# An LSTM on one core: weights in 512 KB transfers, x and h0 behind them, another order of the set-up

## The chip, the cores and the metric

The kernel runs on one core of a Trainium2 chip. The metric is device time in microseconds (us) of one execution. The engines that matter are TensorE (PE in the profile; its weight loads are PEld), VectorE (DVE), ScalarE (ACT), GpSimd (POOL) and SyncE (SP). ACT, SP and POOL also issue DMA transfers, each into a queue of its own[...]. SBUF is the core's working memory, PSUM the memory that TensorE adds its products into, HBM the memory that holds inputs and outputs.

## The reference

An LSTM with 512 hidden values runs over 512 time steps for 16 sequences. Its output is added to its input.

```python
xW = jnp.einsum('ntd,dg->ntg', x, Wx) + b          # x: (16, 512, 512), Wx: (512, 2048)

def step(carry, xw_t):
    prev_h, prev_c = carry
    a = xw_t + prev_h @ Wh                          # Wh: (512, 2048)
    i = sigmoid(a[:, :H]); f = sigmoid(a[:, H:2*H])
    o = sigmoid(a[:, 2*H:3*H]); g = tanh(a[:, 3*H:])
    next_c = f * prev_c + i * g
    next_h = o * tanh(next_c)
    return (next_h, next_c), next_h

_, hs = scan(step, (h0, 0), swapaxes(xW, 0, 1))     # h0: cond_1024, (16, 512)
out = x + swapaxes(hs, 0, 1)
```

All data are float32.

## The kernel before

**Layout.** The 2048 gate columns are cut into four blocks of 32 partitions each (index `j`), and the 512 inputs of a product into four chunks of 128 (index `c`). A chunk of `Wx` or `Wh` is a tile slice of 128 partitions x 2048 columns of float32, 1 MB. `Wx` is used as it is. `Wh` is cut into three float16 parts, `wq[0]`, `wq[1]`, `wq[2]`, whose scaled sum is close to the float32 value, so that the recurrent products run in float16.

**Set-up (lines 333 to 466).** The weights are loaded by `load_w` (line 124): four transfers of 256 KB for a chunk of Wh, issued in turn by SP and ACT, and eight of 128 KB for a chunk of Wx, by SP and POOL. POOL's queue has, ahead of its share of Wx, the first tile of x (`load_xs(0, nc.gpsimd)`, eight transfers of 32 KB), h0 (four) and the bias broadcast over partitions (eight). A semaphore is reused after eight transfers of a kind of queue, and the ninth is issued only when the first has landed.

`bound(c)` finds, for each partition, a bound of the absolute values of chunk `c` of Wh, on DVE for chunks 0 to 2 (line 381) and on ACT for chunk 3 (line 379, an absolute value with a running sum). `scales(h)` makes the scale factors of chunks 2h and 2h + 1 in small DVE operations. `split(n, k)` works on half chunk `n` (0 to 7), in five operations: k = 0, ACT makes the first part (line 414); k = 1, DVE its remainder `r1` (line 417); k = 2, ACT the second part (line 421); k = 3, DVE the remainder `r2` (line 424); k = 4, ACT the third part (line 426). The scheduler is manual: each engine executes its instructions in the order in which the program writes them, and waits where a semaphore says so.

`turn_x(q)` transposes the x of two time steps (a pair, `q`) on DVE. `put_bias(q)` copies the bias into a PSUM bank `xb` on ACT (line 154). `project(q, c)` adds the product with chunk `c` of Wx there on TensorE (line 163). `seed(t, h)` scales the projected values of step `t` from `xb` into the PSUM bank of its gates, on ACT (line 173). `zeros` (line 368) is a product of zeros: 8 of them clear the PSUM banks at the start, and 16 stand as fillers after the first projections.

**Order around the change.** On DVE the transposes of x pairs 0 and 1 and of h0 stand first, then `bound(0)`, `bound(1)`, `scales(0)` and the splits; `bound(2)` is at n = 1, `bound(3)` and `scales(1)` at n = 2. In each pass of the loop over `n`, `split(n, 4)` is the last operation. The two bias copies are at n = 3 and 4, the projections of pairs 0 and 1 at n = 4 in PE's order, the seeds of step 0 at n = 6.

**Steps (lines 468 to 503).** Step 0 uses float32 products with Wh (`first_products`, line 199), each later one the float16 parts (`products`, line 186), with the order of work written out in `STEP_PE` and `STEP`. Each step also projects half of a pair that is needed two to four steps later.

Of the kernel before, what the change touches and what calls it, by code (L numbers as in the profile page):

```python
# [7 lines left out]
FP = mybir.dt.float32  # L8
# [6 lines left out]
P = 128  # L15
Q = 32
# [15 lines left out]
def lstm_residual(ctx: ExitStack, tc: tile.TileContext, x, h0, wx, wh, b, out):  # L32
# [26 lines left out]
    nc = tc.nc  # L59
    N, T, D = x.shape  # L60
    H = h0.shape[1]
    NJ = H // P
    NK = D // P
    G = 4
    U = P // 2
    GU = G * U
# [8 lines left out]
    const = ctx.enter_context(tc.tile_pool(name="const", bufs=1))  # L75
# [38 lines left out]
    parts = [  # L114
        [const.tile([P, 2, 5 * N], HP, tag=f"parts{h}{i}", name=f"parts{h}{i}") for i in range(2)]
        for h in range(2)
    ]
    gates = [
        [psum.tile([P, G * P], FP, tag=f"g{h}{i}", name=f"gates{h}{i}") for i in range(2)]
        for h in range(2)  # L120
    ]
    xb = [psum.tile([P, G * P], FP, tag=f"xb{i}", name=f"xb{i}") for i in range(NXB)]

    def load_w(dst, w, c, dmas, parts=1):


        n = G * H // parts
        for j in range(NJ):
            r0 = j * P + c * Q
            for e in range(parts):  # L130
                a = parts - 1 - e
                dmas[j % 2].dma_start(  # L132
                    out=dst[j * Q : (j + 1) * Q, c, a * n : (a + 1) * n],
                    in_=w[r0 : r0 + Q, e * n : (e + 1) * n],
                )

    xs = {}

    def load_xs(s, dma=nc.sync):

        xs[s] = xsp.tile([P, XP, P], FP, tag="xs", name=f"xs_{s}")
        for j in range(NJ):
            for r in range(S2):
                p0 = j * Q + r * N
                dma.dma_start(
                    out=xs[s][p0 : p0 + N],
                    in_=x[:, s * XB + r : (s + 1) * XB : S2, j * P : (j + 1) * P],
                )
# [4 lines left out]
    def put_bias(q):  # L153
        nc.scalar.copy(xb[q % NXB], bias)  # L154

    def turn_x(q):
        s, i = divmod(q, XP)
        xT[q] = xtp.tile([P, NK, Q], FP, tag="xT", name=f"xT_{q}")
        nc.vector.transpose(xT[q].rearrange("p c m -> p (c m)"), xs[s][:, i])

    def project(q, c):
        for j in range(NJ):
            nc.tensor.matmul(  # L163
                xb[q % NXB][j * Q : (j + 1) * Q],
                lhsT=xT[q][:, c],
                rhs=wx_j[:, c, j],
                start=False,
                stop=(c == NK - 1),
                skip_group_check=True,
            )  # L170

    def seed(t, h):
        nc.scalar.mul(  # L173
            gates[h][t % 2][:, :GU].rearrange("p (g u) -> p g u", g=G),
            xb[t // 2 % NXB].rearrange("p (g h u) -> p h g u", g=G, h=2)[:, h],
            mask[:, t % 2 : t % 2 + 1],
        )
# [155 lines left out]
    h_in = work.tile([P, P], FP, tag="h_in", name="h_in", bufs=1)  # L333
    hT0 = work.tile([P, NK, Q], FP, tag="hT0", name="hT0", bufs=1)
    warm = const.tile([1, 1], FP, tag="warm", name="warm")
    for c in range(NK):
        load_w(wh_sb, wh, c, (nc.sync, nc.scalar))
    load_xs(0, nc.gpsimd)
    nc.vector.memset(zero, 0.0)
    nc.vector.memset(h_in, 0.0)  # L340
    for j in range(NJ):
        nc.gpsimd.dma_start(out=h_in[j * Q : j * Q + N], in_=h0[:, j * P : (j + 1) * P])
    b_j = b.rearrange("(o e g j w) -> j e o g w", o=1, e=2, g=2, j=NJ)
    for j in range(NJ):
        for e in range(2):
            nc.gpsimd.dma_start(
                out=bias[j * Q : (j + 1) * Q, (1 - e) * GU : (2 - e) * GU].rearrange(
                    "p (g w) -> p g w", g=2
                ),
                in_=b_j[j, e].broadcast_to([Q, 2, P]),  # L350
            )
    for c in range(NK):
        load_w(wx_sb, wx, c, (nc.sync, nc.gpsimd), 2)
    load_xs(1)

# [11 lines left out]
    def zeros(bank, start):  # L367
        nc.tensor.matmul(  # L368
            bank, lhsT=zero[:, :P], rhs=zero, start=start, stop=start, skip_group_check=True
        )  # L370


    for bank in xb + gates[0] + gates[1]:
        zeros(bank, True)

    def bound(c):
        if c == NK - 1:
            junk = tmp.tile([P, G * H], HP, tag="junk", name="junk", bufs=1)
            nc.scalar.activation(junk, wh_sb[:, c], AF.Abs, accum_out=amax[:, c : c + 1])  # L379
        else:  # L380
            nc.vector.tensor_reduce(
                amax[:, c : c + 1],
                wh_sb[:, c],
                mybir.AxisListType.X,
                ALU.max,
                apply_absolute_value=True,
            )

    def scales(h):


        nc.vector.tensor_tensor(
            top[:, h : h + 1], amax[:, 2 * h : 2 * h + 1], amax[:, 2 * h + 1 : 2 * h + 2], ALU.max
        )
        t = top[:, h : h + 1].bitcast(I32)
        e, inv = bits[:, h, 0:1], bits[:, h, 1:2]
        nc.vector.tensor_scalar(
            inv.bitcast(I32), t, EXP, EXP, ALU.bitwise_and, ALU.bitwise_xor
        )
        nc.vector.tensor_scalar(e.bitcast(I32), t, EXP, None, ALU.bitwise_and)  # L400
        nc.vector.tensor_scalar(RS2[h], inv, 2.0**12, 0.5, ALU.mult, ALU.min)
        nc.vector.tensor_scalar(RS[h], inv, 2.0**13, 1.0, ALU.mult, ALU.min)
        nc.vector.tensor_scalar(S[h], e, 2.0**-14, 1.0, ALU.mult, ALU.max)
        nc.vector.tensor_scalar(RSL[h], RS[h], 1.0 / LO, None, ALU.mult)
# [3 lines left out]
    def split(n, k):  # L408

        c, e = divmod(n, 2)  # L410
        w = wh_sb[:, c, e * GH : (e + 1) * GH]
        f = [q[:, c, (1 - e) * GH : (2 - e) * GH] for q in wq]
        if k == 0:
            nc.scalar.mul(f[0], w, RS2[c // 2])
        elif k == 1:
            r1[n] = tmp.tile([P, GH], FP, tag="r1", name=f"r1_{n}")
            nc.vector.scalar_tensor_tensor(  # L417
                r1[n], w, RS[c // 2], f[0], ALU.mult, ALU.subtract
            )
        elif k == 2:  # L420
            nc.scalar.copy(f[1], r1[n])  # L421
        elif k == 3:
            r2[n] = tmp.tile([P, GH], FP, tag="r2", name=f"r2_{n}")
            nc.vector.tensor_tensor(r2[n], r1[n], f[1], ALU.subtract)  # L424
        else:
            nc.scalar.mul(f[2], r2[n], LO)  # L426

    NH = 2 * NK
    for q in range(2):
        turn_x(q)  # L430
    nc.vector.transpose(hT0.rearrange("p c m -> p (c m)"), h_in)
    bound(0)
    bound(1)
    scales(0)
    split(0, 0)
    split(1, 0)
    split(0, 1)
    for n in range(NH):
        if n == 1:
            bound(2)  # L440
        if n == 2:
            bound(3)
            scales(1)
        if n + 1 < NH:
            split(n + 1, 1)
        split(n, 2)
        split(n, 3)
        if n + 2 < NH:
            split(n + 2, 0)
        split(n, 4)  # L450
        if n in (3, 4):
            put_bias(n - 3)
        if n == 4:
            for c in range(NK):
                for q in range(2):
                    project(q, c)

            for _ in range(16):
                zeros(xb[3], False)
        if n == 6:  # L460
            for h in range(2):
                seed(0, h)
    for h in range(2):
        seed(1, h)
    put_bias(2)
    turn_x(2)

    for t in range(T):
        s, ti = divmod(t, XB)
        q, half = divmod(t + 4, 2)  # L470
# [12 lines left out]
        for op in STEP.split():  # L483
            name, h = op.split("_")
# [47 lines left out]
```

## Time and profile before

| | us |
|---|---|
| median of 3 runs (lowest, highest) | 2313.13 (2312.34, 2313.43) |
| profiled execution: its own time | 2313.33 |
| profiled execution: span | 2311.4 |
| busy in the span: PE, DVE, ACT, POOL | 2249.4, 1952.7, 1840.0, 136.1 |
| first projection that PE does not interrupt again | starts at 55.60 |
| last of Wh, first tile of x, last of Wx landed | 24.9, 22.6, 45.9 |
| one time step later on (matmuls of line 186 and 163) | 4.36 |

Times are from the start of the span, which is the first instruction of the program. The profile's page is a summary of one execution: busy time of each engine, the span in 40 slices with the busy share in tenths, the DMA queues (q1 is SP's, q10 is ACT's, q0 is POOL's), the chain of work that ended last, and the costliest groups of instructions. The trace behind it can be asked for a stretch: the chain in order of time, the timeline of instructions, or the DMA traffic by queue. In a timeline the value in brackets is how long the engine was idle before the instruction, and what ended it. "Record" is one matmul as the trace has it; a float32 product of `project` leaves two.

### The profile page before, as it was taken

The page shows a single profiled execution, that of the slowest core. Times are in us where ns is not written, and L with a number is a line of the kernel's source. Part 1 is how long each engine was busy: PE and PEld are TensorE (multiplying, and loading weights), DVE is VectorE, ACT ScalarE, POOL GpSimd, SP SyncE. Part 2 cuts the span into 40 slices and gives each one's busy share as a digit, 9 for nine tenths or more (in the row PEclk, how much of TensorE's full clock was granted, in tenths as well). Part 3 has the DMA queues.
Part 4 walks back from the last instruction along what each step waited for, and adds up shares of the span by engine and source line. Part 5 has one row for each costly group of instructions (what it writes and reads, how often), then busy time and mean ns, then how long its engine had stood idle before and what let it go on. Part 6 is the DMA issues. An engine that isn't in the chain of part 4 may idle for free.

```text
span 2311.4 us, 137693 instructions
## 1 busy us (share of the span) xinstructions
PE 2249.4 (97%) x57400; PEld 1572.5 (68%) x57400; DVE 1952.7 (84%) x11812; ACT 1840.0 (80%) x7962; POOL 136.1 (6%) x300
## 2 busy tenths in 40 slices
PE   1999999999999999999999999999999999999997
PEld 0677667766776677667776776677767776777675
DVE  4688888888888888888888888888888888888887
ACT  4788888888888888888888888888888888888887
POOL 3000000000000000000000000000000000000000
PEclk9999999999999999999999999999999999999999
DMA  7000000000000000000000000000000000000000
GB/s 164 4 21 22 14 21 22 13 22 22 13 22 22 13 22 19 16 22 20 15 22 19 16 22 17 18 22 17 18 22 15 20 22 14 21 22 13 22 17 12
DMA packets 84974, 51.10 MB, mean 22 GB/s; under 512 B 17473, under 2 KB 82561, under 8 KB 83841
## 3 DMA queue, kind: packets, MB, share of 16 engines
q1 hardware_dynamic: 82432, 37.52, 7.1%
q8 instruction: 452, 7.41, 1.4%
q0 software_dynamic: 1408, 2.66, 0.6%
q10 hardware_dynamic: 512, 2.13, 0.4%
q14 instruction: 170, 1.38, 0.2%
HBM read 25.46 MB, written 16.78 MB: 18 GB/s over the span
## 4 chain that ended last, share of the span: by engine, by line
PE 97%; DMA 2%; DVE 0%; ACT 0%; issue 0%; ACTq 0%; POOLq 0%; POOL 0%; SPq 0%
PE gates L186 58%; PE xb L163 38%; DMA wh_sb<-in_L_cond_Wh_dram 1%; DMA wx_sb<-in_L_cond_Wx_dram 1%; DMA xs<-in_x_dram 0%; PE gates L199 0%; PE xb L368 0%; DVE r L424 0%; ACT wq L426 0%; ACT junk L379 0%; ACT wq L421 0%; DVE r L417 0%; DVE gt L222 0%; ACT xb L154 0%; ACTq L132 0%
## 5 line engine op out<-in xcount | busy, mean ns | idle before, releaser
L186 PEld LDWEIGHTS <-parts 128*32 128x32 f16 x49056 | 1307.0, 96 | 368.7 <-DVE parts L282 297.9
L186 PE MATMUL gates<-wq,parts 128*32 128x256 f16 x49056 | 1449.0, 273 | 4.2 <-DVE parts L282 4.1
L163 PE MATMUL xb<-wx_sb,xT 128*32 128x512 f32 x8192 | 978.0, 594 | 48.9 <-ACT xb L154 48.9
L222 DVE STREAM_TRANSPOSE gt<-gates 128x192 f32<-128x192 f32 x1024 | 391.8, 383 | 233.0 <-PE gates L186 170.3
L163 PEld LDWEIGHTS xb<-wx_sb,xT 128*32 128x32 f32 x8192 | 264.1, 110 | 355.4 <-issue 303.8
L256 ACT ACTIVATE gc<-pre 128x32 f32<-128x32 f32 x1022 | 234.4, 229 | 274.3 <-DVE pre L229 261.1
L173 ACT ACTIVATE gates<-xb,mask 128x256 f32<-128x256 f32 x1024 | 450.3, 440 | 1.1 <-PE xb L163 1.1
L264 ACT ACTIVATE os<-so,sc 128x32 f32<-128x32 f32 x1024 | 328.9, 321 | 16.7
L286 ACT COPY parts<-parts 128x32 f16<-128x32 f16 x1022 | 214.3, 210 | 131.9 <-DVE parts L282 131.9
L229 DVE SCALAR_TENSOR_TENSOR pre<-gt 128x96 f32<-128x96 f32 x1024 | 253.7, 248 | 0.0
L258 ACT ACTIVATE sif<-pre 128x64 f32<-128x64 f32 x1024 | 245.6, 240 | 0.0
L324 POOL TENSOR_TENSOR ob<-hb,xs 128x128 f32<-128x128 f32 x256 | 116.8, 456 | 2149.6 <-DVE hb L323 1909.6
L222 DVE STREAM_TRANSPOSE gto<-gates 128x64 f32<-128x64 f32 x1024 | 229.6, 224 | 0.0
L274 ACT ACTIVATE tch<-gc 128x32 f32<-128x32 f32 x1024 | 226.6, 221 | 0.2
L262 ACT ACTIVATE so<-preo 128x32 f32<-128x32 f32 x1024 | 226.4, 221 | 0.0
L296 DVE SCALAR_TENSOR_TENSOR parts<-rem,parts 128x32 f16<-128x32 f32 x1022 | 196.2, 192 | 35.5
L229 DVE SCALAR_TENSOR_TENSOR preo<-gto 128x32 f32<-128x32 f32 x1024 | 192.2, 188 | 17.6
L288 DVE SCALAR_TENSOR_TENSOR parts<-parts,hist 128x32 f16<-128x32 f16 x1022 | 191.9, 188 | 17.7
L266 DVE TENSOR_TENSOR pr<-sif,gc 128x64 f32<-128x64 f32 x1022 | 204.7, 200 | 0.0
L282 DVE TENSOR_TENSOR parts<-os,tch 128x32 f16<-128x32 f32 x1022 | 196.4, 192 | 0.0
L272 DVE TENSOR_TENSOR gc<-pr 128x32 f32<-128x32 f32 x1024 | 192.2, 188 | 0.0
L276 DVE SCALAR_TENSOR_TENSOR hist<-os,tch 128x32 f32<-128x32 f32 x1024 | 188.8, 184 | 0.3 <-ACT tch L274 0.3
(45 smaller groups left out, 741.2 us busy)
## 6 DMA issues: line engine op xcount, KB each, us to landing
xs<-in_x_dram SPq DMA_DIRECT2D x504, 32.0 KB, 2.2
out_dram<-ob SPq DMA_DIRECT2D x504, 32.0 KB, 1.9
wh_sb<-in_L_cond_Wh_dram ACTq DMA_DIRECT2D x8, 256.0 KB, 10.6
wh_sb<-in_L_cond_Wh_dram SPq DMA_DIRECT2D x8, 256.0 KB, 10.6
wx_sb<-in_L_cond_Wx_dram SPq DMA_DIRECT2D x16, 128.0 KB, 5.9
wx_sb<-in_L_cond_Wx_dram POOLq DMA_DIRECT2D x16, 128.0 KB, 6.8
xs<-in_x_dram POOLq DMA_DIRECT2D x8, 32.0 KB, 13.2
bias<-in_L_cond_b_dram POOLq DMA_DIRECT2D x8, 32.0 KB, 5.5
```

The costliest lines, as they stand in the source:

```text
L163: nc.tensor.matmul(xb[q % NXB][j * Q : (j + 1) * Q], lhsT=xT[q][:, c], rhs=wx_j[:, c, j], start=False, stop=(c == NK - 1), skip_group_chec ...
L173: nc.scalar.mul(gates[h][t % 2][:, :GU].rearrange("p (g u) -> p g u", g=G), xb[t // 2 % NXB].rearrange("p (g h u) -> p h g u", g=G, h=2)[: ...
L186: nc.tensor.matmul(g[j * Q : (j + 1) * Q, :GU], lhsT=a[:, cc, k * N : (k + 2) * N], rhs=wq_j[i - 1][:, 2 * kh + cc, h, j], start=False, st ...
L222: nc.vector.transpose(gt.rearrange("p b m -> p (b m)"), gates[h][t % 2][:, b0 * Q : b1 * Q])
L229: nc.vector.scalar_tensor_tensor(pre.rearrange("p g (c n) -> p (g c) n", c=2), gt[:, :, (1 - t % 2) * N : (2 - t % 2) * N], 1.0 / LO, gt[: ...
L256: nc.scalar.activation(gc[h][:, 0], v["pre", h][:, 0], AF.Tanh)
L258: nc.scalar.activation(new("sif", t, h, [P, 2, 2 * N]), v["pre", h][:, 1:3], AF.Sigmoid)
L262: nc.scalar.activation(new("so", t, h, [P, 2 * N]), v["preo", h][:, 0], AF.Sigmoid)
L264: nc.scalar.mul(new("os", t, h, [P, 2 * N]), v["so", h], S[h])
L266: nc.vector.tensor_tensor(new("pr", t, h, [P, 2, 2 * N]), v["sif", h], gc[h], ALU.mult)
L274: nc.scalar.activation(new("tch", t, h, [P, 2 * N]), gc[h][:, 1], AF.Tanh)
L286: nc.scalar.copy(slots(t, h, 2), slots(t, h, 0))
```

## The change

`load_w` now loads two chunks with one call: for Wh eight transfers of 512 KB in all (a transfer holds a block of 32 partitions with two rows each), for Wx sixteen of 256 KB. Blocks j = 0, 1 go through the first queue given, j = 2, 3 through the second. x's first tile and h0 move from POOL's queue to SP's, behind Wh and ahead of SP's Wx. POOL loads a row of the bias first, and then the bias tile and its Wx.

The banks `xb[0]` to `xb[2]` get their bias by 24 products of a row of ones with the bias row, instead of a product of zeros and, later, a copy on ACT. From pair 3 on `put_bias` is used as before.

`bound(1)` moves to ACT (it has the running sum there), `bound(3)` to DVE. `bound(2)` moves ahead by one pass. `split(n, 4)` is issued one pass later, after `split(n + 1, 3)`. The transposes of x (pairs 0 to 2) and of h0 move from the front of DVE's order to the end of pass n = 3. The steps' code is unchanged.

```diff
-    def load_w(dst, w, c, dmas, parts=1):
+    def load_w(dst, w, c0, dmas, parts=1):
         n = G * H // parts
-        for j in range(NJ):
-            r0 = j * P + c * Q
-            for e in range(parts):
-                a = parts - 1 - e
-                dmas[j % 2].dma_start(
-                    out=dst[j * Q : (j + 1) * Q, c, a * n : (a + 1) * n],
-                    in_=w[r0 : r0 + Q, e * n : (e + 1) * n],
-                )
+        for j in range(2):
+            for q, dma in enumerate(dmas):
+                r = w[(2 * q + j) * P + c0 * Q :][: 2 * Q].rearrange("(c u) f -> u c f", u=Q)
+                p = slice((2 * q + j) * Q, (2 * q + j + 1) * Q)
+                for e in range(parts):
+                    a = parts - 1 - e
+                    dma.dma_start(
+                        out=dst[p, c0 : c0 + 2, a * n : (a + 1) * n],
+                        in_=r[:, :, e * n : (e + 1) * n],
+                    )
...
-    for c in range(NK):
+    brow = const.tile([1, G * H], FP, tag="brow", name="brow")
+    ones = const.tile([1, Q], FP, tag="ones", name="ones")
+    for c in (0, 2):
         load_w(wh_sb, wh, c, (nc.sync, nc.scalar))
-    load_xs(0, nc.gpsimd)
+    load_xs(0)
     nc.vector.memset(zero, 0.0)
     nc.vector.memset(h_in, 0.0)
+    nc.vector.memset(ones, 1.0)
     for j in range(NJ):
-        nc.gpsimd.dma_start(out=h_in[j * Q : j * Q + N], in_=h0[:, j * P : (j + 1) * P])
+        nc.sync.dma_start(out=h_in[j * Q : j * Q + N], in_=h0[:, j * P : (j + 1) * P])
+    nc.gpsimd.dma_start(out=brow, in_=b.rearrange("(o f) -> o f", o=1))
...
-    for c in range(NK):
+    for c in (0, 2):
         load_w(wx_sb, wx, c, (nc.sync, nc.gpsimd), 2)
...
-    for bank in xb + gates[0] + gates[1]:
+    for bank in gates[0] + gates[1] + xb[3:]:
         zeros(bank, True)
+    for bank in xb[:3]:
+        for e in range(2):
+            for j in range(NJ):
+                nc.tensor.matmul(
+                    bank[j * Q : (j + 1) * Q, (1 - e) * GU : (2 - e) * GU],
+                    lhsT=ones,
+                    rhs=brow.rearrange("p (e g j w) -> p e j g w", e=2, g=2, j=NJ)[:, e, j],
+                    start=(e == 0),
+                    stop=False,
+                    skip_group_check=True,
+                )
...
-        if c == NK - 1:
+        if c == 1:
             junk = tmp.tile([P, G * H], HP, tag="junk", name="junk", bufs=1)
...
-    for q in range(2):
-        turn_x(q)
-    nc.vector.transpose(hT0.rearrange("p c m -> p (c m)"), h_in)
     bound(0)
     bound(1)
     scales(0)
     split(0, 0)
+    split(0, 1)
     split(1, 0)
-    split(0, 1)
     for n in range(NH):
-        if n == 1:
+        if n == 0:
             bound(2)
         if n == 2:
             bound(3)
             scales(1)
         if n + 1 < NH:
             split(n + 1, 1)
         split(n, 2)
         split(n, 3)
+        if n:
+            split(n - 1, 4)
         if n + 2 < NH:
             split(n + 2, 0)
-        split(n, 4)
-        if n in (3, 4):
-            put_bias(n - 3)
+        if n == 3:
+            for q in range(3):
+                turn_x(q)
+            nc.vector.transpose(hT0.rearrange("p c m -> p (c m)"), h_in)
...
+    split(NH - 1, 4)
     for h in range(2):
         seed(1, h)
-    put_bias(2)
-    turn_x(2)
```

## The prediction

> **What bounds the kernel now.** The page's first two parts say that TensorE is full from about slice 2 on, at full clock; the recurrence is its own bound.
>
> ```profile
> PE 2249.4 (97%) x57400; PEld 1572.5 (68%) x57400; DVE 1952.7 (84%) x11812; ACT 1840.0 (80%) x7962; POOL 136.1 (6%) x300
> PE   1999999999999999999999999999999999999997
> ```
>
> None of the 511 later time steps is edited, so only the set-up ahead of them can move. The chain of waits in order of time (start us, us, what) shows where it ends:
>
> ```profile
> 54.01 1.06 ACT wq L426
> 55.06 0.49 ACT xb L154
> 55.60 8.32 PE xb L163 x56
> 63.92 4.18 PE xb L368 x16
> 68.10 6.29 PE gates L199 x128
> 74.39 1.72 PE xb L163 x16
> ```
>
> From 55.60 on PE hardly rests again. What stood last before it is ACT's bias copy, queued behind the Wh splits. So the end moves by as much as the end of `first_products` (74.39) moves, and I compute that one time. The timeline (start, us, engine, line, [idle before <- releaser]) says why the splits were late:
>
> ```profile
> 22.68 0.50 DVE L159 STREAM_TRANSPOSE xT<-xs 128x128 f32<-128x128 f32 x2 [20.65 <-DMA xs<-in_x_dram]
> 26.15 0.31 DVE L431 STREAM_TRANSPOSE hT<-h_in 128x128 f32<-128x128 f32 x1 [2.97 <-DMA h_in<-in_cond_dram]
> 26.39 4.45 DVE L381 TENSOR_REDUCE amax<-wh_sb 128x1 f32<-128x2048 f32 x2
> 50.20 1.06 ACT L426 ACTIVATE wq<-r 128x1024 f16<-128x1024 f32 x1 [0.24 <-DVE r L424]
> 54.01 1.06 ACT L426 ACTIVATE wq<-r 128x1024 f16<-128x1024 f32 x1 [0.24 <-DVE r L424]
> ```
>
> DVE sat until 26.1 for x and h0, although the trace's landings have Wh's chunks 0 and 1 at 14.4 and all of Wh at 24.9. After that each half chunk took 3.8 us (50.20 to 54.01), as ACT waits on DVE for `split(n, 4)`. Behind these stands the transfer of Wx, hidden today: its last piece lands at 45.9.
>
> [...] In 36 to 44 us POOL's Wx (two 4 KB pieces per engine and transfer) ran against SP's x (four of 512 B):
>
> ```profile
> q0 software_dynamic: 467, 1.29, 82.4%
> q1 hardware_dynamic: 786, 0.32, 26.7%
> ```
>
> 1.29 against 0.32 MB is 4 to 1, the ratio of whole transfers per engine and not of pieces (8 to 1). [...] here the sum stays at 201 to 251 GB/s in the stretches 2 to 24, 24 to 30, 30 to 36 and 36 to 44 us, whoever issues. [...] projection records are 0.214 us apart from 55.60 to 59.9 and 0.107 us after; in `first_products` 0.053 us until 73.5 and 0.027 after.
>
> **The change, part by part.**
>
> *Wh's arrival.* 4.19 MB now goes as eight transfers of 512 KB, all issued at once. Before, 4.64 MB moved in 2 to 24 us (211 GB/s). POOL's queue again holds small transfers meanwhile (8 KB of bias row and 8 of 32 KB, where it had 8 x transfers of 32 KB), so I put chunks 0 and 1 at 13.5 and chunks 2 and 3 at 24.0 (23 to 25).
>
> *Bounds and splits.* DVE no longer waits for x and h0. The reduction of chunk 0 (2.2) runs beside ACT's of chunk 1 (1.89 + 0.19), and `scales(0)` and the first split operations are done by about 20. Then `bound(2)` stands in DVE's order ahead of `split(1, 1)`, and waits for the second half of Wh: all of DVE is queued behind it, and ACT's `split(1, 2)` with it. From 24.0 DVE runs, in its new order: two reductions at 2.2, `scales(1)` at 0.7, four r1 at 1.19 (line 417), four r2 at 1.14 (line 424), 14.4 in all. The first `turn_x` ends at 24.0 + 14.4 + 0.3 = 38.7. ACT keeps up: `split(n - 1, 4)` now uses an r2 made one half earlier, and three ACT operations at about 1.0 make 3.0 us per half where it was 3.8. ACT reaches `seed(0, ...)` at about 46.5. Its last splits stand behind the seeds and end near 52; step 1's products want them after 59, so they cost nothing. Were that cover gone, they would cost up to 3 us.
>
> *Bias by products.* Two copies of 0.49 leave the path, a third was off it. The 24 small matmuls need only a row of the bias, and run in PE's idle time (some 20 us before 38); unhidden they would be 48 records at 0.05 to 0.11 (the 0.053 of 128 columns at half clock, up to doubled for 256), 2.4 to 5.3 us. The row is POOL's first transfer; the first of x there landed at 9.9 today. I take nothing. The `ones` memset is a row of 32 values among idle DVE time.
>
> *x, h0 and Wx.* x[4..7] wait for landings of Wh's second half, h0[0..3] for x[0..3], SP's first four Wx pieces for x[4..7], the last four for h0. So SP's Wx stands behind 0.26 MB of x and 0.03 MB of h0 in short pieces. Against POOL's Wx, x took 8 us for 0.32 MB above[...]. I put the start of SP's Wx at 31 to 36. POOL's half flows from about 25 with the rest of the bandwidth. What is left after 24 us is 4.19 + 0.29 = 4.5 MB; at 251 to 201 GB/s it ends between 42 and 46.4, so 45. The half that projection's chunks 0 and 1 need from SP (1.05 MB) lands at 39.5 (start 31, shared at 125) to 41.3 (start 36, alone at 200): I take 40.3.
>
> *PE.* It starts at the later of 38.7 and 40.3: 40.3. Projection of pairs 0 and 1 is 8 + 56 = 64 records. [...] 24 x 0.214 + 40 x 0.107 = 9.4, ending at 49.7 (8.6 to 10.3 with the ends). Chunks 2 and 3 are wanted at 45.4 or later, so their landing at 45 is just hidden; each us beyond 46 costs a us. Seeds need the projection of pair 0 only and end under the 16 filler products, as before. Fillers and `first_products` took 4.18 + 6.29 = 10.5, nearly all of the second at half clock; fully warm they would take 16 x 0.217 + 128 x 0.027 = 6.9. [...] I take 9.4. `first_products` ends at 59.1.
>
> *Sum.* 74.4 - 59.1 = 15.3 us. The profiled execution took 2313.33 (span 2311.4 and 1.9 around it), near the median of 2313.13. 2313.3 - 15.3 = 2298.0.
>
> **Rivals.**
>
> *The forecast* (0.67): end of `first_products` at 59.1, own range from start 39.5, 8.6 and 8.0 (56.1) to start 41.5, 10.3 and 10.5 (62.3): 2295.0 to 2301.2.
>
> *Wx becomes the bound* (0.15): POOL's half runs first, SP's then goes alone through one queue from 38 at 150 GB/s, and lands at 52. Then the last 32 records (3.4 warm, 6.9 if the clock fell) and 9.4 follow: 65 to 68, so 2304 to 2307; smaller delays make 2301 to 2304. For it: x and h0 stand ahead of SP's Wx. Against: one queue with POOL's bias beside it moved 184 GB/s (page of 24 to 30 us: 1.11 MB in 6 us).
>
> *More is won* (0.10): PE starts by 39[...], and `first_products` runs warm: 39 + 8.6 + 6.9 = 54.5, a gain of 19.9, 2293.4; about 2291 to 2295.
>
> *Nothing measurable* (0.05): the gain is eaten where Wx's last piece lands at 57 (57 + 3.4 + 9.4 = 69.8, under 4.6 us won). That is 4.5 MB at 136 GB/s, below every stretch of the trace before 44 us.
>
> *Slower* (0.03): SP's chain of waits serialises. If x, h0 and Wx, 20 transfers, went one after the other at the 2.2 us from issue to landing that the page has for x, the last would land at 24 + 44 = 68, and `first_products` would end at 68 + 3.4 + 9.4 = 80.8: 2319.7. It decides from a last landing of 66 on. Against: eight semaphores go round, so up to eight are in flight, as today.
>
> **How the numbers follow.** 0.2% (4.6 us) is about what this measurement can tell from no change. The forecast, the larger gain and the late Wx are all faster by more: 0.92; same 0.05; slower 0.03. The range of 2293.0 to 2304.5 holds the forecast's 0.67, about 0.07 of the larger gain and 0.08 of the late Wx.
>
> **What would show it.** Right: the first reduction starts at 13 to 15, the reduction of chunk 2 at 23 to 25, xT at 38 to 40; PE's first projection at 39.5 to 41.5 without a wait on ACT; ACT's line 444 waits no longer for DVE by 0.24; `first_products` ends at 56 to 62, and the steps after it take 4.36 us each as now. Wrong: a PE wait on Wx between projection records, Wh's second half after 27 (POOL's Wx cutting in), SP idle between its Wx pieces, or a change in the later steps, which I hold at nothing because neither their instructions nor their order are touched.

## The result and the profile after

The changed kernel takes 2297.58 us (median of 6 runs, 2294.09 to 2298.14), the kernel before 2313.06 beside it: a ratio of 0.9931, 95% interval 0.9918 to 0.9944, or 15.5 us won. The forecast was 2298.0.

The execution that was profiled is the fastest of the six: 2294.09, span 2291.7. Its granted clock is 0.999 over the span, and 0.998 in the five others; that difference becomes the main theme of the first experiments. The first two parts of its page:

```profile
PE 2249.4 (98%) x57445; PEld 1572.7 (69%) x57445; DVE 1952.7 (85%) x11813; ACT 1838.1 (80%) x7959; POOL 127.2 (6%) x281
PE   4999999999999999999999999999999999999997
```

PE is busy for the same 2249.4 us as before, in a span that is 19.7 us shorter. So what went is, on balance, idle time, in the first slice (4 tenths busy instead of 1). The chain of waits in order of time:

```profile
22.44 9.42 DMA xs<-in_x_dram
31.86 0.02 issue
31.88 6.03 DMA wx_sb<-in_L_cond_Wx_dram
37.91 0.14 issue
38.05 9.27 PE xb L165 x64
47.31 3.56 PE xb L374 x16
50.87 3.63 PE gates L201 x128
54.50 1.72 PE xb L165 x16
```

What stands last before PE's unbroken run is now a transfer of Wx at 37.9, no longer ACT's bias copy at 55.1. `first_products` (L201) ends at 54.5 instead of 74.4. From the first `products` of step 2 to the end of the span it is 2231.1 us (2291.7 - 60.55), against 2230.9 before (2311.4 - 80.45): the steps did not change.

DVE's timeline shows where the time came from:

```profile
12.77 2.29 DVE L399 TENSOR_REDUCE amax<-wh_sb 128x1 f32<-128x2048 f32 x1 [10.69 <-DMA wh_sb<-in_L_cond_Wh_dram]
22.26 2.29 DVE L399 TENSOR_REDUCE amax<-wh_sb 128x1 f32<-128x2048 f32 x1 [4.07 <-DMA wh_sb<-in_L_cond_Wh_dram]
...
36.79 0.69 DVE L161 STREAM_TRANSPOSE xT<-xs 128x128 f32<-128x128 f32 x3
```

The first reduction starts at 12.8 instead of 26.4, with the landing of Wh's first half. DVE then waits once more, for Wh's second half, and works without a break to the transposes of x at 36.8. Between 24 and 32 us the DMA view has POOL's Wx against SP's x and h0:

```profile
q0 software_dynamic: 439, 1.41, 86.5%
q1 hardware_dynamic: 531, 0.28, 20.4%
```

POOL's queue took five times the bytes of SP's. Its last piece of Wx landed at 33.2, all of x at 31.9 and h0 at 33.5, and only then came SP's share of Wx, one 256 KB piece every 1.28 us to the last at 43.2.

### The profile page after: what moved, and what is told of

It reads as the page before. It is cut to its first block, busy times and chain, and to the rows that moved or that the text cites. A ratio compares the mean times of both kernels' runs of the same rounds, so it can differ in the third digit from the quotient of the medians.

```text
span 2291.7 us, 137735 instructions
## 1 busy us (share of the span) xinstructions
PE 2249.4 (98%) x57445; PEld 1572.7 (69%) x57445; DVE 1952.7 (85%) x11813; ACT 1838.1 (80%) x7959; POOL 127.2 (6%) x281
## 4 chain that ended last, share of the span: by engine, by line
PE 98%; DMA 2%; DVE 0%; issue 0%; ACTq 0%; POOLq 0%; POOL 0%; SPq 0%
PE gates L188 59%; PE xb L165 38%; DMA wh_sb<-in_L_cond_Wh_dram 1%; DMA xs<-in_x_dram 0%; DMA wx_sb<-in_L_cond_Wx_dram 0%; PE gates L201 0%; PE xb L374 0%; ACTq L134 0%; DVE gt L224 0%; DVE preo L231 0%; DVE pre L231 0%; DVE parts L284 0%; DVE gto L224 0%; POOLq L544 0%; POOL ob L326 0%
## 5 line engine op out<-in xcount | busy, mean ns | idle before, releaser
L188 PEld LDWEIGHTS <-parts 128*32 128x32 f16 x49056 | 1307.1, 96 | 368.8 <-DVE parts L284 298.8
L188 PE MATMUL gates<-wq,parts 128*32 128x256 f16 x49056 | 1449.2, 273 | 4.2 <-DVE parts L284 4.2
L258 ACT ACTIVATE gc<-pre 128x32 f32<-128x32 f32 x1022 | 234.7, 230 | 274.7 <-DVE pre L231 261.9
```

Source lines behind the costliest of these rows:

```text
L188: nc.tensor.matmul(g[j * Q : (j + 1) * Q, :GU], lhsT=a[:, cc, k * N : (k + 2) * N], rhs=wq_j[i - 1][:, 2 * kh + cc, h, j], start=False, st ...
L258: nc.scalar.activation(gc[h][:, 0], v["pre", h][:, 0], AF.Tanh)
```

## The experiments

There are twelve experiments. e1 to e4, e5 to e8 and e9 to e12 were each measured beside runs of the kernel before, whose medians were 2312.9, 2315.41 and 2315.06; so kernels of different groups are compared by their ratio to it. They are told here by the question that they answer.

### The clock: fillers and the first step's products

**e1, the changed kernel again**, without an edit.

> The changed kernel again, unedited, to see whether its profiled execution (2294.09, below its median of 2297.58) differs from the others in the clock. Clock theory: most executions fall back to half clock while the 16 filler products run, so that first_products takes about 6.3 us instead of 3.6; median 2297.6, and a profile of such an execution has first_products at 5 to 6.3 us and its end near 58, all else as in the first profile. Start theory: the spread comes from the start of the projections (38 in the first profile, 41 in others), with first_products at 3.6 in each.

Median 2296.81 (2295.65 to 2298.84), ratio 0.9931 (0.9918 to 0.9943). The profile is now of the slowest execution, 2298.84. Its chain:

```profile
37.63 9.77 PE xb L165 x64
47.40 4.42 PE xb L374 x16
51.82 6.05 PE gates L201 x128
57.87 1.72 PE xb L165 x16
```

The projections start 0.4 earlier than in the first profile and end at 47.4, as there. The same 16 fillers then took 4.42 instead of 3.56, and the same 128 records of `first_products` 6.05 instead of 3.63. In the kernel before these two rows are 4.18 and 6.29, and its granted clock is 0.50 from 66.7 to 73.5, over the last fillers and most of `first_products`; in the first profile it is 1.00 from 47.3 to 54.5. Of the 3.9 us between the two spans 3.3 are in these two rows (10.47 against 7.19). In the kernel before, the records of `first_products` were 0.053 us apart at half clock and 0.027 after it; with that factor of two I estimate, from the 3.3 us, about 6.6 us of half clock in e1. The clock theory holds, the start theory falls.

**e2, no fillers.**

```diff
-            for _ in range(16):
-                zeros(xb[3], False)
```

> The changed kernel without the 16 filler products of zeros, which only pass time. In the first profile the seeds of step 0 end at 47.3, with the projections, so nothing has to be waited for. Clock theory: 3.6 us of fillers go, and first_products always runs at full clock, which most executions lack: end near 51, median 2290.5 (7 below 2297.6). Start theory: only the 3.6 us go: 2294.0. Rival on the fillers: they cover a wait for the seeds, the time stays within 1 us of 2297.6.

Median 2291.07 (2290.63 to 2291.28), ratio 0.9905 (0.9892 to 0.9919): 5.7 below e1, nearer to the clock theory's 7 than to the 3.6 of the other, and with a spread of 0.7 us instead of 3.2. ACT's timeline shows the rest:

```profile
49.17 1.06 ACT L444 ACTIVATE wq<-r 128x1024 f16<-128x1024 f32 x1 [0.33 <-DVE r L442]
50.14 0.79 ACT L175 ACTIVATE gates<-xb,mask 128x256 f32<-128x256 f32 x2
50.85 0.23 ACT L258 ACTIVATE gc_init<-pre 128x32 f32<-128x32 f32 x1
```

The first activation of step 0 (L258) comes directly behind the last split and the seeds of step 1, with no idle time: ACT's order is now the bound, and step 1's products (L188) begin at 52.38 after 0.26 of waiting. This is the cover that the prediction named for the last splits.

**e3, fillers over 128 rows.**

```diff
+    zfull = const.tile([P, G * P], HP, tag="zfull", name="zfull")
...
+    nc.vector.memset(zfull, 0.0)
...
-                zeros(xb[3], False)
+                nc.tensor.matmul(
+                    xb[3], lhsT=zfull[:, :P], rhs=zfull, start=False, stop=False,
+                    skip_group_check=True,
+                )
```

> The changed kernel with 16 fillers that multiply zeros over 128 rows instead of one row (same columns, same number). Clock theory with the row count as its cause: [...] first_products at full clock in every execution, median 2294.1, less spread. If zeros of any shape do not count, or if the clock is not the cause: 2297.6.

Median 2294.57 (2294.36 to 2295.38), ratio 0.9921 (0.9908 to 0.9935). Every run is below the lowest of e1. The chain:

```profile
47.55 3.56 PE xb L479 x16
51.11 3.63 PE gates L202 x128
```

Same number, same columns, still only zeros; yet the two rows take 3.56 and 3.63 us, where e1's took 4.42 and 6.05, and the granted clock over the span is 0.999 in each of the five runs, where three of e1's have 0.998. The fillers of the two kernels differ in their rows, one in e1 and 128 here; what in the hardware makes the difference was not shown.

**e4, the kernel before without fillers** (the same two lines deleted there).

> The kernel before without its 16 fillers. In its profile they took 4.18 us and first_products 6.29 at half clock, seeds done at 64.0 and projections at 63.9. Clock theory: 4.1 of the fillers and 2.8 of first_products go: 2306.1. Start theory: 4.1 go: 2309.0. Fillers cover a wait: 2313.

Median 2308.1 (2307.46 to 2309.07), ratio 0.9979 (0.9971 to 0.9988): 4.8 won, where 6.9 (clock) or 4.1 (start) were expected. PE's timeline shows why it lies between:

```profile
63.10 3.67 PE L199 MATMUL gates<-wh_sb,hT 128*32 128x128 f32 x128
67.93 1.92 PE L163 MATMUL xb<-wx_sb,xT 128*32 128x512 f32 x16 [1.17 <-ACT xb L154]
```

`first_products` did run at full clock (3.67 instead of 6.36), but the projection of pair 2 behind it then waited 1.17 us for that pair's bias copy, which stands behind ACT's last split and seeds.

### Loads or order

**e5, order only.** The changed kernel with the loads of before: `load_w` by chunk as before, and

```diff
-    load_xs(0)
+    load_xs(0, nc.gpsimd)
...
-        nc.sync.dma_start(out=h_in[j * Q : j * Q + N], in_=h0[:, j * P : (j + 1) * P])
+        nc.gpsimd.dma_start(out=h_in[j * Q : j * Q + N], in_=h0[:, j * P : (j + 1) * P])
```

> The changed kernel with the loads of before (Wh in 256 KB and Wx in 128 KB transfers by chunk, x and h0 by POOL), so only the order on the engines and the bias products are changed. Order theory: the loads bring little; Wh is complete at 24.9 instead of 22.1, xT 14.7 later at 39.6, projections start at 39.7 instead of 38.05, Wx's last chunk at 46 just in time: 2299 (1.7 above the changed kernel's 2297.3). Loads theory: the gain needs the large transfers, or x and h0 behind Wh: 2305 or more.

Median 2299.71 (2298.95 to 2300.86), ratio 0.9935 (0.9922 to 0.9947): nearly the whole gain, and not to be told from the 0.9931 of the whole change. On top of the new order, the new transfers brought nothing measurable. The path was not the one that I expected, as PE's timeline shows:

```profile
37.13 3.64 PE L163 MATMUL xb<-wx_sb,xT 128*32 128x512 f32 x16 [4.78 <-DMA wx_sb<-in_L_cond_Wx_dram]
...
44.27 1.92 PE L163 MATMUL xb<-wx_sb,xT 128*32 128x512 f32 x16 [0.99 <-DMA wx_sb<-in_L_cond_Wx_dram]
```

PE starts with the first chunks of Wx and stands again for the later ones. With single chunks `bound(2)` has to wait for chunk 2 alone (landed at 20.1), so DVE has xT at 35.7 already, earlier than in the changed kernel. But Wx arrives chunk by chunk and late, and projections end at 49.8 instead of 47.3.

**e6, loads only.** The kernel before with the changed `load_w`, and x and h0 through SP.

> The kernel before with the loads of the change (512 and 256 KB transfers, x and h0 by SP behind Wh) and nothing else. Order theory: DVE's order has the transposes of x and h0 first, and these land at 31.9 and 33.5 now; the first reduction starts at 33.9 instead of 26.4 and all after it is 7.5 later: 2320.4, slower than before. Loads theory: Wh's first half at 12.6 and its whole at 22.1 are worth something by themselves: 2310.

Median 2322.31 (2321.59 to 2323.44), ratio 1.0033 (1.0020 to 1.0045): 6.9 us slower than before, where 7.4 were expected. DVE's timeline:

```profile
32.48 0.50 DVE L161 STREAM_TRANSPOSE xT<-xs 128x128 f32<-128x128 f32 x2 [30.45 <-DMA xs<-in_x_dram]
34.21 0.31 DVE L433 STREAM_TRANSPOSE hT<-h_in 128x128 f32<-128x128 f32 x1 [1.22 <-DMA h_in<-in_cond_dram]
34.44 4.44 DVE L383 TENSOR_REDUCE amax<-wh_sb 128x1 f32<-128x2048 f32 x2
```

All of Wh lies in SBUF from 21.9 on, and DVE waits behind the transposes of x and h0, which want data from the end of the queue: the first reduction is 8.0 us later than before.

**e11, transposes first.** The changed kernel with one thing undone.

```diff
+    for q in range(2):
+        turn_x(q)
+    nc.vector.transpose(hT0.rearrange("p c m -> p (c m)"), h_in)
     bound(0)
...
-        if n == 3:
-            for q in range(3):
-                turn_x(q)
-            nc.vector.transpose(hT0.rearrange("p c m -> p (c m)"), h_in)
...
         seed(1, h)
+    turn_x(2)
```

> The changed kernel with the transposes of x pairs 0 and 1 and of h0 back in front of the first reduction on DVE. Order theory (this place is the change's main part): DVE waits for h0 until 33.5, the first reduction starts at 33.8 instead of 12.8, the seeds come at 61.2, first_products runs from 62.0 at half clock to 68.3, 10.4 after the 57.9 of a common execution: ratio 0.9976. Rival: other parts carry the gain (Wh's second half at 22 sets the pace in any case, with 11 us of DVE's delay made up): 0.9945 or less.

Median 2309.22 (2308.33 to 2309.85), ratio 0.9974 (0.9964 to 0.9984), against 0.9931 of the changed kernel: with the new transfers, about 10 us of the gain hang on this place. DVE's timeline, then PE's:

```profile
33.23 0.31 DVE L449 STREAM_TRANSPOSE hT<-h_in 128x128 f32<-128x128 f32 x1 [2.01 <-DMA h_in<-in_cond_dram]
33.47 2.24 DVE L399 TENSOR_REDUCE amax<-wh_sb 128x1 f32<-128x2048 f32 x1
...
37.77 9.70 PE L165 MATMUL xb<-wx_sb,xT 128*32 128x512 f32 x64 [22.41 <-DMA wx_sb<-in_L_cond_Wx_dram]
47.41 4.56 PE L374 MATMUL xb<-zero 1*128 1x512 f16 x16
61.31 6.46 PE L201 MATMUL gates<-wh_sb,hT 128*32 128x128 f32 x128 [9.35 <-ACT gates L175]
```

The projections are as early as ever, as x comes before Wx. What is late is ACT: its splits wait for DVE's, the seeds come at 60.84, and PE stands for 9.35 us.

e6 and e11 also tell what the rest is worth. Both have the new transfers and these transposes in front; e11 has besides the later `split(n, 4)`, the bias products and the other places of the bounds. Their ratios are 1.0033 and 0.9974, about 13 us apart. So the place of the transposes is not the whole of the order's gain.

### The smaller parts

**e7, bias copies.** The changed kernel with the 24 products taken out and `put_bias(n - 3)` at the end of passes 3 and 4, `put_bias(2)` at the end.

> The changed kernel with the bias of pairs 0 to 2 copied by ACT as before (copies at the end of passes 3 and 4 and after the splits) instead of products. Path theory: the projections of pair 0 start at 40.1 behind ACT's splits, those of pair 1 wait for their copy until 43.1; projections end at 50.5 instead of 47.3: 2300.5. Rival: the copies hide beside the wait for Wx: 2297.3.

Median 2297.67 (2296.83 to 2300.64), ratio 0.9926 (0.9913 to 0.9940): no difference that can be told from 0.9931. PE's timeline:

```profile
38.12 1.93 PE L165 MATMUL xb<-wx_sb,xT 128*32 128x512 f32 x8 [33.34 <-DMA wx_sb<-in_L_cond_Wx_dram]
40.78 7.90 PE L165 MATMUL xb<-wx_sb,xT 128*32 128x512 f32 x56 [0.73 <-ACT xb L156]
```

I had put ACT one half chunk too late. The first copy is done by 37.3, under the wait for Wx; the second holds PE for 0.73, and projections end at 48.7 instead of 47.3. That 1.3 us is smaller than the 3.2 us of spread in e1.

**e8, `split(n, 4)` early.**

```diff
-        if n:
-            split(n - 1, 4)
         if n + 2 < NH:
             split(n + 2, 0)
+        split(n, 4)
...
-    split(NH - 1, 4)
```

> The changed kernel with split(n, 4) back at the end of pass n, behind split(n + 2, 0). Path theory: ACT waits for DVE's r2 in each half again, a half takes 3.8 us instead of 3.0; xT comes at 40.2, projections start at 40.3, and ACT reaches the seeds at 53.8, 1 us after the fillers: first_products starts 3.5 later, 2300.8. Rival: the last operation was off the path: 2297.3.

Median 2295.97 (2295.77 to 2297.88), ratio 0.9920 (0.9908 to 0.9933): again not to be told from 0.9931. ACT's timeline has the waits that I expected, and PE's what hides them:

```profile
38.65 1.06 ACT L444 ACTIVATE wq<-r 128x1024 f16<-128x1024 f32 x1 [0.24 <-DVE r L442]
41.93 1.06 ACT L444 ACTIVATE wq<-r 128x1024 f16<-128x1024 f32 x1 [0.24 <-DVE r L442]
...
49.46 0.80 ACT L175 ACTIVATE gates<-xb,mask 128x256 f32<-128x256 f32 x2
```

```profile
38.89 8.48 PE L165 MATMUL xb<-wx_sb,xT 128*32 128x512 f32 x64 [23.19 <-DVE xT L161]
50.86 5.37 PE L201 MATMUL gates<-wh_sb,hT 128*32 128x128 f32 x128
```

A half chunk takes 3.28 us on ACT (38.65 to 41.93) instead of 2.93, xT comes at 38.5 instead of 36.8. The 3.8 that I expected was misread: in the kernel before, a bias copy stands between the two lines that I took it from (50.20 and 54.01).

```profile
46.92 1.06 ACT L426 ACTIVATE wq<-r 128x1024 f16<-128x1024 f32 x1 [1.19 <-DVE r L424]
...
50.20 1.06 ACT L426 ACTIVATE wq<-r 128x1024 f16<-128x1024 f32 x1 [0.24 <-DVE r L424]
51.16 0.58 ACT L154 COPY xb<-bias 128x512 f32<-128x512 f32 x1
```

The half ahead of that, without a copy, took 3.28 there too (46.92 to 50.20).

The first half of Wx, landed at 37.4 in e8, hides a part of the delay; PE starts at 38.9, 0.8 to 1.3 after the two profiles of the changed kernel, and ends its projections at the same 47.4, as its 64 records took 8.48 us, against 9.27 and 9.77 in those two. That part is luck. The seeds end at 50.3, still under the fillers.

**e9, x and h0 through POOL**, ahead of its bias row (the two lines of e5, with the large weight transfers kept).

> The changed kernel with x's first tile and h0 back in POOL's queue, ahead of its bias row, bias and Wx. Share theory (the engines' time is what is short, not a queue): SP's Wx starts at 22 and ends near 33[...], POOL's Wx then goes alone: its part of chunks 0 and 1 lands at 39.5, all at 44.5; projections start 1.5 later: ratio to the kernel before 0.9938, 1.5 us above the changed kernel's 0.9931. Place theory (x and h0 ahead of SP's Wx hold the start at 38): start at 36.9 and 0.9926.

Median 2299.89 (2299.01 to 2303.88), ratio 0.9941 (0.9928 to 0.9953); its interval overlaps that of 0.9931, so the time alone doesn't decide. PE's timeline does:

```profile
40.22 5.24 PE L165 MATMUL xb<-wx_sb,xT 128*32 128x512 f32 x32 [8.61 <-DMA wx_sb<-in_L_cond_Wx_dram]
```

SP's Wx is complete at 33.8, POOL's part of chunks 0 and 1 at 40.1, its last at 45.5: the roles are swapped, and the start is 2.2 later. SP's Wx no longer stands behind the small transfers, but POOL's does. The place theory falls.

**e10, bounds as before**: `bound(1)` on DVE and `bound(3)` on ACT again.

```diff
-        if c == 1:
+        if c == NK - 1:
```

> The changed kernel with bound(1) back on DVE and bound(3) back on ACT. Cover theory: the second reduction of 2.2 us fits into DVE's wait for Wh's second half (18.2 to 22.3), and ACT's bound(3) makes scales(1) 1.6 later; xT at 38.4 instead of 36.8, projections at 38.5 instead of 38.05: 0.4 us, ratio 0.9933, not to be told from 0.9931. Rival: two engines at once are worth their 2.2 us: 0.9941.

Median 2299.28 (2298.79 to 2299.89), ratio 0.9932 (0.9920 to 0.9945). The second reduction ran in DVE's wait for Wh, which fell from 4.07 to 1.82 us; xT came at 36.0, not later than in the changed kernel but earlier (36.8 in its first profile, 36.4 in e1's), since behind 22 us DVE is rid of a reduction of 2.3 us and waits 1.7 for ACT's instead. Wx bounds the start all the same (37.8).

**e12, a warm start.** The kernel of e2 with ten products ahead of the projections:

```diff
+            for _ in range(10):
+                nc.tensor.matmul(
+                    xb[3], lhsT=zfull, rhs=wq[0][:, 2, GH : GH + G * P], start=False, stop=False,
+                    skip_group_check=True,
+                )
             for c in range(NK):
```

> The changed kernel without the 16 fillers after the projections, and with 10 products of a zero weight (128 rows) with a finished half chunk of wq[0] ahead of them, from 33.2 on, so that the projections start at full clock. Wx theory: the records then take 0.107 us, but Wx's last chunk at 43.2 ends the gain; projections end at 46.6 instead of 47.3; 0.7 us below the run without fillers (0.9905): 0.9902. Clock theory: the cold stretch of 4.5 us is worth 2.2: 0.9896. Rival: after the fillers ACT's last splits and seeds bound the start of the steps, and nothing is won: 0.9905.

Median 2292.46 (2292.17 to 2292.65), ratio 0.9903 (0.9888 to 0.9918), the same as e2 within the interval. PE's timeline:

```profile
37.72 3.65 PE L166 MATMUL xb<-wx_sb,xT 128*32 128x512 f32 x32 [0.28 <-DMA wx_sb<-in_L_cond_Wx_dram]
42.98 3.64 PE L166 MATMUL xb<-wx_sb,xT 128*32 128x512 f32 x32 [1.60 <-DMA wx_sb<-in_L_cond_Wx_dram]
```

All records run at full clock (32 in 3.65 and in 3.64 us, where the first 32 of e9 took 5.24), and PE then waits 1.60 us for Wx's last piece, landed at 42.8. The half clock at the start of the changed kernel's projections (38.05 to 42.5 in the first profile, with records 0.214 us apart) was hidden by the transfer. ACT, as in e2, works without a break from the seeds of step 1 into the first activation of step 0 (50.56), so a start of the products 0.3 us earlier than in e2 shows nothing in the time.

So e2 is the version to keep: 2291.07, 21.8 us below the kernel before and 5.7 below the changed one, by deleting two lines. Wx's landing and ACT's last splits are its next bounds.

## Why the prediction was right

**The frame held.** The set-up moved, and the span with the end of `first_products`: this end came 19.9 us earlier (74.4 to 54.5) in the first profile, whose span fell by 19.7, and 16.5 earlier (57.9) in e1's, whose span fell by 15.8. The mechanism held as well: the new order on the engines carries the gain (e5), 10 us of it at the place of the transposes (e11), and Wx's landing takes over as the bound.

**The steps of the sum**, forecast against the first profile and e1:

| | forecast | first profile | e1 |
|---|---|---|---|
| Wh's halves landed | 13.5, 24.0 | 12.6, 22.1 | 12.5, 21.7 |
| DVE from there to `turn_x` | 14.4 | 14.5 | 14.5 |
| Wx's first half landed | 40.3 | 37.9 | 37.5 |
| projections start | 40.3 | 38.05 | 37.63 |
| projections take | 9.4 | 9.3 | 9.8 |
| Wx's last piece landed | 45 | 43.2 | 42.7 |
| fillers and `first_products` | 9.4 | 7.2 | 10.5 |
| end of `first_products` | 59.1 | 54.5 | 57.9 |

The start of the projections was the term most off, 2.3 us too late. Two steps failed in it. Wh came 1.9 earlier: I had kept the 211 GB/s of before, and from 2 us to its last landing at 22.1 the DMA engines moved 236 (208 with the transfers of before in e5, from 2 to 25.3 us), although POOL's queue had more to move meanwhile (0.57 MB against 0.36 until Wh had landed before). What in the new transfers makes them faster was not tested. And I took the middle of two pictures for Wx's first half, SP shared from 31 or alone from 36. In fact POOL's share was through by 33.2 and SP's went alone from then on, at 256 KB in 1.28 us (205 GB/s). The rival of a late Wx assumed 150 for that, and fell with it; its premise, that x and h0 hold SP's Wx back until POOL's is done, was true.

The second term off is the clock. I took a middle value of 9.4 for a time that the profiles show as 7.2 (first profile), 8.9 (e8, e9) or 10.5 (e1), with `first_products` at 3.63, 5.30 (e8) and 6.05 of it. That value was my estimate, and so were, for the projections, the 24 of 64 records at half clock (16 and 32 for the ends of the range); no trace of before shows these counts for the new order. In the first profile the records were 0.214 us apart for the first 4.5 us, to 42.5, and 0.107 after; all 64 took 9.27, against 9.77 in e1 and 8.48 in e8. The rival "more is won" was a lower value for the fillers and `first_products`, 6.9, together with an early start, and the first profile is it: 54.5, as worked out there. That the median met the forecast within 0.5 us is partly luck: a start too late and a clock too favourable are errors of opposite sign. In both profiles four of the signs that I named came ahead of their ranges, in the first one at these times: the first reduction 12.8, the reduction of chunk 2 22.3, xT 36.8 and PE's start 38.05.

**Edits costed at nothing.** The bias products took 5.34 us of PE between 10.2 and 15.5, in idle time. The two copies that they replace were counted at 1.0 on the path; e7 shows 1.3. `split(n - 1, 4)` made a half 2.93 us on ACT, where 3.0 was said, but against 3.28 and not against the 3.8 that I read from the lines (see e8), and in e8 no gain from it can be seen in the time: Wx holds most of the start, and the fillers cover the seeds. The cover of ACT's last splits was real: without it (e2) they hold the start of the steps. The slower case by a chain of SP's waits did not come: all eight 256 KB pieces were issued by 33.6, before the first of them landed at 34.1, and they landed 1.26 to 1.42 us apart.

## What to carry to other kernels

An instruction that waits for late data should not stand ahead of work whose data are there, on an engine that executes in the program's order, as DVE did in e6 (Wh landed at 21.9, first reduction at 34.4); and a change of the order of transfers and one of the order on the engines have to be judged together, since here the first alone cost 6.9 us (e6), the second, with the bias products, won without it about as much as both together (0.9935 in e5 against 0.9931). When one wait goes, look up what lands next: three of the parts here (e7, e8, e10) were worth nothing measurable, mostly because Wx's transfer lay over them. That does not make them worthless: with the transposes in front, where ACT's splits bound the start, they were worth about 13 us together (e6 against e11). And products that only pass time are not free: ask whether anything still waits for what they cover.

## What the hardware did that was not expected

TensorE's clock fell back to half while PE was busy without a gap. In the kernel before, PE is busy all the time from 55.60 to 74.4; its granted clock is 1.00 from 59.9 to 66.7, 0.50 from there to 73.5, and 1.00 again to 2305.9. When it fell, the sixteen products over a single row had run since 63.9, for 2.8 us. In e1 these products and `first_products` took 4.42 and 6.05 us; in e3, where the same number went over 128 rows of zeros, 3.56 and 3.63. The medians are 2296.81 and 2294.57. So in these kernels a busy PE was not enough to keep the full clock, and the rows of the fillers, one or 128, went with the difference. Other row counts were not tried, and what decides in the hardware was not shown.

The bias products are over one row as well, and keep PE busy for 5.34 us without a gap. Their records, of 256 columns each, are 0.107 us apart from the first to the last. The projections' records, of 512 columns, are 0.214 apart until 42.5 and 0.107 after, so that the bias products kept, per column, the pace of half clock throughout. In e12 ten products with 128 rows of zero weights took 4.42 us from 33.02 on, and the projections behind them ran at full clock from the start, 32 records in 3.65 us.

The same one-row fillers and `first_products` took different times in different executions:

| profile | 16 fillers | `first_products` |
|---|---|---|
| first profile | 3.56 | 3.63 |
| e5, e8 | 3.55, 3.56 | 5.30, 5.30 |
| e1, e7 | 4.42, 4.59 | 6.05, 5.88 |
| before | 4.18 | 6.29 |

What sets the time of a single execution was not shown.
